# A cross-attention and feed-forward kernel: value matrices placed between score products, weights turned by VectorE in 32x32 blocks

## The chip, the cores and the metric

The kernel runs on one core of one Trainium2 chip. The core has TensorE (PE, whose weight loads are listed apart as PEld), VectorE (DVE), ScalarE (ACT), GpSimd (POOL) and SyncE (SP), and 16 DMA engines that SP, ACT and POOL feed through queues. Time is device microseconds of one execution; the figure is the median of three runs.

## The reference

`x` is 4 batches of 1024 tokens of 512 numbers; `ctx` is 64 context tokens per batch. 16 heads of 64. All is float32.

```python
# attention part, h = layernorm(x)
q, k, v = heads(h @ w_q), heads(ctx @ w_k), heads(ctx @ w_v)
scores = q @ k.T / 8 + causal(-10000)           # 1024 x 64 per head
x = x + tanh(g_xattn) * (softmax(scores) @ v) @ w_o

# feed-forward part, h = layernorm(x); act_qdq: one scale for the whole tensor
h = act_qdq(h)                                  # 16 bits
up   = act_qdq(h @ lpbq(w_up).T)                # w_gate, w_up: 1536 x 512
gate = act_qdq(h @ lpbq(w_gate).T)
gate = act_qdq(gate * u16(sigmoid(gate)))
x = x + tanh(g_ffn) * (act_qdq(gate * up) @ lpbq(w_down).T)
```

`lpbq` takes each run of 32 weights of a row, scales it by its largest absolute value over 7, rounds to integers and scales back.

## The kernel before, in words

**Folding.** The kernel never forms q, k or v of the long side. It computes per batch b a matrix `m_all[b]` (512 x 1024: `w_q` times the keys) and a matrix `vwo[b]` (1024 x 512: values times `w_o`, scaled by tanh). Scores of a token are then its normed row times `m_all[b]`; the attention output is the softmax weights times `vwo[b]`. Each is two halves in two buffers.

**Products by sevens.** The large products take two token tiles (a pair, `q`) at once and a 2x2 split of both sides, in seven products instead of eight. Each side needs sums of its blocks first: of the tokens (`score_left`, L346), of the softmax weights (in `weights_turned`, L616), of `m_all` and `vwo` (`batch_sums(b, k)`, L364: k=0 for `m_all`, k=1 for `vwo`; four DVE operations on 128x1024 numbers, L381 to L386) and of the weights (`weight_sums`, L279).

**Stages.** Set-up loads the weights and computes keys, `m_all` (the loop over head pairs `hp`, with the first pair's tokens turned at hp=7, L482) and values. Then the value-matrix loop (L527): first batches 2 and 3 together, then 0 and 1 together, for each head pair one matrix of each of the two batches, of two 64x64 products on TensorE; the even batch is evicted by ACT (L543), the odd one by DVE (L545). `m_all` and `vwo` of batches 2 and 3 are written to DRAM by POOL (L521, L547) and fetched when needed. `batch_sums(0, 0)` stands before the second round.

Attention is a loop over 16 pairs (L735), four pairs a batch. `scores(q+1)` (L555) runs ahead, seven products into three PSUM banks `sp`, `sq`, `sn`, evicted by ACT and DVE (L576, L578); between them stand the transposes of pair q's softmax weights (L627) and of pair q+2's tokens (L352), by a table `between`/`behind`. Then `softmax(q+1)` on DVE and ACT (L590 to L612), `attend(q)` (L639) with seven products into PSUM tiles `opn` and `oq`, evicted by DVE into the token buffer `xg` (L669, L672, L675), and `renormed` (L680), the second norm with its transposes (L700). After `attend`, at pairs 1 and 3 of a batch, the next batch's `batch_sums` are traced.

In the same loop one chunk (128 rows) of the gate weights per pair is loaded by one DMA from SP and turned into its levels by `dequantized` (L216: reduce, two small steps, two 128x512 products, L221 to L230); chunks 4 to 11 come first and go to DRAM raw (`wg_d`), chunks 0 to 3 stay; pairs 13 and 14 fetch two groups back and prepare four up chunks. The chunks are transposed on TensorE, four 128x128 blocks each (L235), and copied by ACT (L237): gate chunks in pairs 13 to 15, the early up chunks after the last pair, the other eight up chunks in the gate stage.

The gate stage (24 units of seven products, L839, PSUM evicted at L847 to L865 and L956), the up stage, and the down stage (L1448, L1372) follow. A scale over all tokens (`a_x`) stands between attention and gate.

**What sets the order.** Each engine runs its own list in order. The list is made at compile time: a planner takes the earliest traced of the operations that it believes ready, with operations under `high_priority` ahead; TensorE's list follows the source in the attention and gate stages (`manual_schedule`). `keep_in_program_order` puts one operation behind the one traced before it on its engine; `issue_after(ins)` puts a block's operations behind `ins`. Large buffers come from one pool of 20 slots of 8 KB per partition.

```python
ps = ps_mm.tile([P, H], F32, name=f"ps_vo{b}_{hp}", tag="mm")
for j in range(2):
    half = slice(j * D, (j + 1) * D)
    to = j if b % 2 == 0 else 1 - j
```

Here `half` is the half of TensorE's rows that a product reads and `to` the half of its columns that it fills; an even and an odd batch use different quarters.

Of the kernel before, what the change touches and what calls it, by code (L numbers as in the profile page):

```python
# [7 lines left out]
F32 = mybir.dt.float32  # L8
I16 = mybir.dt.int16
# [8 lines left out]
P = 128  # L18
# [9 lines left out]
def kernel(  # L28
# [123 lines left out]
    wg_d = [dram.tile([P, 4, H], F32, name=f"wg_d{k}") for k in range(2)]  # L152
# [63 lines left out]
    def dequantized(pool, src, w, name, in_order=False):  # L216

        nc.sync.dma_start(out=w, in_=src)
        wb = w.rearrange("p (n k) -> p n k", k=QB)
        am = pool.tile([P, NQB], F32, name=f"wam_{name}", tag="wam")  # L220
        ins = nc.vector.tensor_reduce(am, wb, AX.X, ALU.max, apply_absolute_value=True)  # L221
        if in_order:
            tc.keep_in_program_order(ins)
        nc.vector.tensor_scalar(am, am, 1.0 / W_QMAX, 1e-12, ALU.mult, ALU.max)
        inv = pool.tile([P, NQB], F32, name=f"winv_{name}", tag="winv")
        nc.vector.reciprocal(inv, am)
        shape = [P, NQB, QB]
        wi = pool.tile(shape, I16, name=f"wi_{name}", tag="wi", bufs=1)
        nc.vector.tensor_tensor(wi, wb, inv.unsqueeze(2).to_broadcast(shape), ALU.mult)
        nc.vector.tensor_tensor(wb, wi, am.unsqueeze(2).to_broadcast(shape), ALU.mult)  # L230
# [10 lines left out]
    wgT, wuT, wd, wdT, up_chunks = [], [], [], [], []  # L241

    def turned_chunk(psp, w, oc, into, name):

        if oc % 4 == 0:
            into.append(slot([P, HC, 4 * P], f"w{name}T{oc // 4}"))
        cols = slice((oc % 4) * P, (oc % 4 + 1) * P)
        ps = psp.tile([P, 4, P], F32, name=f"wps_{name}{oc}", tag="tr")
        turned(ps, w, into[-1][:, :, cols])

    def up_chunk(psp, w):
        oc = len(up_chunks)
        up_chunks.append(oc)
        turned_chunk(psp, w, oc, wuT, "u")
# [133 lines left out]

    with tc.tile_pool(name="su", bufs=1) as su, tc.tile_pool(
# [88 lines left out]
        for hp in range(HP):  # L478
            if hp + 1 < HP:
                query_turned(hp + 1)  # L480
            else:
                left[0] = score_left(0, centred(0))  # L482
# [40 lines left out]

# [3 lines left out]
        for a in reversed(range(B // 2)):  # L527
            if a == 0:
                for _ in batch_sums(0, 0):
                    pass  # L530
            for hp in range(HP):
                for b in (2 * a, 2 * a + 1):
                    ps = ps_mm.tile([P, H], F32, name=f"ps_vo{b}_{hp}", tag="mm")
                    for j in range(2):
                        half = slice(j * D, (j + 1) * D)
                        to = j if b % 2 == 0 else 1 - j
                        nc.tensor.matmul(
                            ps[to * D : (to + 1) * D, :], vT[half, hp, b * KL : (b + 1) * KL],
                            wo[hp // 4][half, hp % 4, :], start=True, stop=True,
                        )  # L540
                    dst = vwo[b][hp // 4][:, hp % 4, :]
                    if b % 2 == 0:
                        nc.scalar.activation(dst, ps, AF.Copy, scale=tanh_g[0])  # L543
                    else:
                        nc.vector.tensor_scalar(dst, ps, tanh_g[0], None, ALU.mult)  # L545
                    if b > 1 and hp % 4 == 3:
                        nc.gpsimd.dma_start(out=vwo_d[b][hp // 4], in_=vwo[b][hp // 4])  # L547
# [3 lines left out]
    with tc.tile_pool(name="ps_s", bufs=1, space=PSUM) as ps_s, tc.tile_pool(  # L551
# [3 lines left out]
        def scores(q, between):  # L555

            a, b = left.pop(q), right[0][q // QPB]
            e = pa.tile([P, 2, NH, KL], F32, name=f"e{q}", tag="e")
            c = e.rearrange("p i (n h) k -> p i n (h k)", n=2)
            bank = {  # L560
                k: ps_s.tile([P, H], F32, name=f"{k}{q}", tag=k) for k in ("sp", "sq", "sn")
            }
            m1, c12, c22 = c[:, 1, 0], c[:, 0, 1], c[:, 1, 1]
            for k, at, start, dst, other in (
                (1, "sp", True, m1, None), (6, "sq", True, c12, m1), (2, "sp", False, c[:, 0, 0], None),
                (5, "sn", True, c22, m1), (7, "sq", False, c22, c22), (3, "sn", False, c12, c12),
                (4, "sq", False, m1, m1),
            ):
                for h in range(HC // 2):
                    nc.tensor.matmul(  # L570
                        bank[at], a[k][:, h, :], b[k][:, h, :],
                        start=start and h == 0, stop=h == HC // 2 - 1, skip_group_check=True,
                    )
                with tc.high_priority(SOON):
                    if other is None:
                        nc.scalar.copy(dst, bank[at])  # L576
                    else:
                        nc.vector.tensor_tensor(dst, bank[at], other, add)  # L578
                if k in between:
                    between[k]()  # L580
            return e

        def softmax(q, e):

            for i in range(2):
                t = 2 * q + i
                ei = e[:, i]

                if t % TPB == 0:
                    nc.vector.tensor_tensor(  # L590
                        ei, ei, cmask.unsqueeze(1).to_broadcast([P, NH, KL]), ALU.add
                    )
                mx = pa.tile([P, NH], F32, name=f"mx{t}", tag="mx")
                nc.vector.tensor_reduce(mx, ei, AX.X, ALU.max)
                sm = pa.tile([P, NH], F32, name=f"sm{t}", tag="sm")
                if q == 0:

                    nc.vector.tensor_tensor(
                        ei, ei, mx.unsqueeze(2).to_broadcast([P, NH, KL]), ALU.subtract
                    )  # L600
                    nc.scalar.activation(ei, ei, AF.Exp)
                    nc.vector.tensor_reduce(sm, ei, AX.X, ALU.add)
                else:
                    nc.vector.tensor_scalar(mx, mx, -1.0, None, ALU.mult)  # L604
                    for h in range(NH):
                        nc.scalar.activation(  # L606
                            ei[:, h, :], ei[:, h, :], AF.Exp, bias=mx[:, h : h + 1],
                            accum_out=sm[:, h : h + 1],
                        )
                rs = pa.tile([P, NH], F32, name=f"rs{t}", tag="rs")  # L610
                nc.vector.reciprocal(rs, sm)
                nc.vector.tensor_tensor(  # L612
                    ei, ei, rs.unsqueeze(2).to_broadcast([P, NH, KL]), ALU.mult
                )
# [24 lines left out]
        def attend(q, a):  # L639
# [15 lines left out]
            for k, at, start, dst in (  # L655
# [9 lines left out]
                with tc.high_priority(SOON):  # L665
                    if k == 1:
                        nc.scalar.copy(r, bank[at])
                    else:
                        nc.vector.tensor_tensor(dst, bank[at], dst, add)  # L669
# [8 lines left out]
            finished(2 * q, x1)  # L678

# [32 lines left out]
        sg_t, ag, early_up, gate_raw = [], [], [], []  # L712
# [7 lines left out]
        def made_ready(ws, n, src, name, first=0, in_order=False):  # L720

            oc = (len(ws) + first) % n
            if oc % 4 == 0:
                made_in.append(slot([P, min(4, n - oc), H], f"w_{name}{oc}"))
            w = made_in[-1][:, oc % 4, :]
            dequantized(pa, src[oc * P : (oc + 1) * P, :], w, f"{name}{oc}", in_order)
            ws.append(w)

        made_in = []
        two = centred(1)  # L730
        ahead = scores(0, {3: lambda: next_left(1)})
        softmax(0, ahead)
        for _ in batch_sums(0, 1):
            pass
        for q in range(NQ):  # L735
# [15 lines left out]
            if q + 1 < NQ:  # L751
                a = []
                behind = {3: lambda: next_left(q + 2)}
                if q > 0:
                    behind = {5: turn, 3: lambda: (a.append(turn()), next_left(q + 2))}
                ahead = scores(q + 1, behind)
                softmax(q + 1, ahead)
            if q == 0 or q + 1 == NQ:
                turn()
                a = [turn()]  # L760
# [7 lines left out]

            j = q - (NQ - IC // 4)
            if j >= 0:  # L770
                for oc in range(4 * j, 4 * j + 4):
                    turned_chunk(ps_tr, gate_raw[oc], oc, wgT, "g")
# [3 lines left out]
            attend(q, a[0])  # L776
            if b + 1 < B and k in (1, QPB - 1):
                for _ in batch_sums(b + 1, k // 2):
                    pass
# [725 lines left out]
```

## Time and profile before

| | |
|---|---|
| median of 3 runs (lowest, highest) | 1469.0 us (1468.91, 1469.15) |
| the profiled execution | 1467.07 us |
| its span, first to last instruction | 1465.3 us |
| PE, DVE, ACT, POOL busy | 97%, 77%, 47%, 7% |
| TensorE clock granted, mean | 0.995 |
| DMA: moved, mean rate | 240.12 MB, 164 GB/s |
| DMA packets, of them under 512 B | 74,168, 7,396 |

A group's line names the source line, the engine, the operation, out<-in with the count, busy time and mean of one, and the idle time before it with what ended it. A timeline's line gives start and length, the same names, and in brackets the wait before it. TensorE's operations overlap: a group's length holds the tail of its last one, so costs are read from start to next start. A 128x128 transpose is one TensorE instruction, any other float32 product two.

### The profile page before, as it was taken

The numbers are of one execution on the slowest core, as the hardware profiler recorded it, in microseconds if no ns is written. First come the engines' busy times: TensorE is split into PE (matmuls) and PEld (weight loads), VectorE is DVE, ScalarE is ACT, GpSimd is POOL, SyncE is SP. The second block draws the span as 40 slices with busy tenths as digits, with TensorE's granted clock in tenths as the row PEclk, the third lists the DMA queues.
The fourth block names the chain that finished last, engine by engine and source line by source line (L and its number), as shares of the span: only waits on it lengthen the run. The fifth ranks groups of instructions, "written<-read, shape, count | busy, mean of one in ns | idle before, by whom it ended". The sixth has DMA issues, their size and how long they took to land. (4 is left out here: it accounts for less than half of the span.)

```text
span 1465.3 us, 15463 instructions
## 1 busy us (share of the span) xinstructions
PE 1417.2 (97%) x5040; PEld 869.3 (59%) x5040; DVE 1128.0 (77%) x2059; ACT 693.4 (47%) x1746; POOL 96.6 (7%) x191
## 2 busy tenths in 40 slices
PE   8898999999999998999999999999999899999999
PEld 6545766766676674444444444444444448888887
DVE  2976887977988779899956569988888897666632
ACT  2645867767678673111000049977776532222200
POOL 0100000000000001000000000000000101111110
PEclk9999999999999999999999999999999999999999
DMA  9630231431312133664322439958557475554321
GB/s 330 244 130 15 72 115 72 159 129 58 130 47 110 46 130 158 236 223 187 129 86 102 157 127 345 373 216 316 212 210 267 164 282 174 187 187 172 143 72 43
DMA packets 74168, 240.12 MB, mean 164 GB/s; under 512 B 7396, under 2 KB 7652, under 8 KB 68068
## 3 DMA queue, kind: packets, MB, share of 16 engines
q1 hardware_dynamic: 48612, 137.39, 26.8%
q0 software_dynamic: 18560, 76.56, 13.4%
q10 hardware_dynamic: 6912, 25.17, 4.3%
q8 instruction: 39, 0.64, 0.2%
q14 instruction: 45, 0.37, 0.1%
HBM read 130.03 MB, written 109.05 MB: 163 GB/s over the span
## 5 line engine op out<-in xcount | busy, mean ns | idle before, releaser
L606 ACT ACTIVATE e<-e,mx 128x64 f32<-128x64 f32 x480 | 159.7, 339 | 2.2 <-DVE mx L604 2.1
L839 PE MATMUL pqup<-t,wuT 128*128 128x512 f32 x192 | 92.3, 603 | 5.2 <-DVE raw_up L860 2.6
L606 ACT ACTIVATION_READ_ACCUMULATOR e<-e,mx 128x1 f32 x480 | 92.3, 192 | 0.0
L839 PE MATMUL pqgate<-t,wgT 128*128 128x512 f32 x192 | 90.2, 592 | 0.0
L855 ACT COPY raw_gate<-ppgate 128x512 f32<-128x512 f32 x24 | 14.0, 585 | 145.5 <-PE ppgate L839 145.5
L1372 PE MATMUL ep<-wdT,upe 128*128 128x256 f32 x336 | 77.1, 379 | 0.0
L1298 ACT ACTIVATE uie<-upe,inv_up 128x1024 int16<-128x1024 f32 x48 | 53.8, 1145 | 45.8 <-DVE upe L1302 28.7
L661 PE MATMUL oq<-t,eT 128*128 128x256 f32 x256 | 63.7, 393 | 12.0 <-DVE xg L669 8.1
L1372 PE MATMUL eq<-tw,upe 128*128 128x256 f32 x312 | 72.4, 379 | 0.0
L1372 PEld LDWEIGHTS ep<-wdT,upe 128*128 128x128 f32 x336 | 63.8, 190 | 9.1 <-issue 0.5
L1071 ACT ACTIVATE gi<-gt,inv_gate 128x1024 int16<-128x1024 f32 x48 | 54.9, 1143 | 30.3 <-DVE q L1081 30.0
L839 PEld LDWEIGHTS pqup<-t,wuT 128*128 128x128 f32 x192 | 34.7, 189 | 57.0 <-issue 29.7
L839 PE MATMUL ppgate<-xh,wgT 128*128 128x512 f32 x144 | 67.7, 592 | 0.0
L839 PE MATMUL ppup<-xu,wuT 128*128 128x512 f32 x144 | 67.7, 592 | 0.0
L1372 PEld LDWEIGHTS eq<-tw,upe 128*128 128x128 f32 x312 | 59.3, 190 | 8.1
L839 PEld LDWEIGHTS pqgate<-t,wgT 128*128 128x128 f32 x192 | 36.3, 190 | 46.1 <-issue 37.9
L1302 DVE SCALAR_TENSOR_TENSOR upe<-uie,inv_o,gse 128x1024 f32<-128x1024 int16 (+1 forms) x50 | 60.4, 1231 | 3.3 <-ACT uie L1298 3.0
L661 PEld LDWEIGHTS oq<-t,eT 128*128 128x128 f32 x256 | 49.4, 195 | 21.9 <-DVE xg L669 11.0
L570 PE MATMUL sq<-t,xs 128*128 128x512 f32 x128 | 60.3, 593 | 0.0
L629 ACT COPY eT<-ps_e 128x512 f32<-128x512 f32 x64 | 34.3, 588 | 53.5 <-PE ps_e L627 53.5
L967 DVE TENSOR_REDUCE am_gate<-raw_gate 128x1 f32<-128x1024 f32 x48 | 58.2, 1213 | 0.9
L1103 ACT ACTIVATE ar<-raw_up 128x1024 f32<-128x1024 f32 x46 | 48.2, 1047 | 19.1 <-DVE raw_up L1029 19.1
(353 smaller groups left out, 3141.2 us busy)
## 6 DMA issues: line engine op xcount, KB each, us to landing
gate_d<-raw_gate ACTq DMA_DIRECT2D x48, 512.0 KB, 2.6
gt<-gate_d SPq DMA_DIRECT2D x48, 512.0 KB, 4.8
upe<-up_d SPq DMA_DIRECT2D x24, 1024.0 KB, 5.9
up_d<-raw_up POOLq DMA_DIRECT2D x46, 512.0 KB, 3.5
gse<-gsi_d SPq DMA_DIRECT2D x24, 512.0 KB, 4.6
gsi_d<-q SPq DMA_DIRECT2D x44, 256.0 KB, 4.0
xg<-in_x_dram SPq DMA_DIRECT2D x8, 1024.0 KB, 5.2
x_d<-xg POOLq DMA_DIRECT2D x32, 256.0 KB, 2.3
```

The lines of the kernel that those rows point to most:

```text
L570: nc.tensor.matmul(bank[at], a[k][:, h, :], b[k][:, h, :], start=start and h == 0, stop=h == HC // 2 - 1, skip_group_check=True,)
L606: nc.scalar.activation(ei[:, h, :], ei[:, h, :], AF.Exp, bias=mx[:, h : h + 1], accum_out=sm[:, h : h + 1],)
L629: nc.scalar.copy(eT[:, 2 * i + k], ps)
L661: nc.tensor.matmul(bank[at], a[k][:, h, :], b[k][:, h, :], start=start and h == 0, stop=h == HP // 2 - 1, skip_group_check=True,)
L839: nc.tensor.matmul(bank[at], a[k][:, h, :], b[k][:, h, :], start=start and h == 0, stop=h == HC // 2 - 1, skip_group_check=True,)
L855: nc.scalar.copy(r0[:, 0, :], bank["pp"])
L967: nc.vector.tensor_reduce(am_gate[:, u : u + 1], rf, AX.X, ALU.max, apply_absolute_value=True)
L1071: nc.scalar.activation(gi, g, AF.Copy, scale=inv_g)
L1103: nc.scalar.activation(ar, raw[u], AF.Abs)
L1298: nc.scalar.activation(ui, up[:, i, :], AF.Copy, scale=inv_u)
L1302: ins = nc.vector.scalar_tensor_tensor(o[:, i, w], ui[:, w], c_o, gs[:, i, w], ALU.mult, ALU.mult)
L1372: nc.tensor.matmul(bank[at], a[u // 2][k][:, u % 2, q % 2, :], w_of[u // 2][k][:, u % 2, :], start=start and u == 0, stop=u == UPB - 1, sk ...
```

## The change

Three edits, made together.

**Weights.** `turned_chunk` loads a chunk of gate or up weights straight into its place in the turned buffer, by 16 DMAs from SP, each of 32 partitions and runs of 32 numbers, so that 32x32 blocks lie already where their transposed blocks belong; `levels` (the former body of `dequantized`) works on them there, and one DVE transpose, which turns each block of 32x32 in place, ends it. The TensorE transposes and ACT copies of gate and up chunks are gone, also in the gate stage, where the eight up chunks are now at units 2 to 9 instead of 0 to 7. `wg_d` holds turned groups. The down weights are as before.

**Value matrices.** The loop in the set-up makes those of batches 2 and 3 only, with the first pair's tokens turned at hp=2 and `batch_sums(0, 0)` ahead of it. Those of batch 0 are made two at a time behind products 6, 2, 5 and 7 of `scores(0)`, those of batch 1 behind products 1, 6, 2 and 5 of `scores(1)`, in the PSUM tiles that `attend` uses. ACT evicts all but every second one of batch 3. `next_left(1)` moves behind `softmax(0)`; the first pair's softmax weights are turned behind products 3 and 4 of `scores(1)`; `batch_sums(0, 1)` is cut in two, ahead of `softmax(0)` and behind `softmax(1)`.

**Sums.** `batch_sums` after `attend` is issued behind the last eviction of `attend`.

```diff
-    wg_d = [dram.tile([P, 4, H], F32, name=f"wg_d{k}") for k in range(2)]
+    wg_d = [dram.tile([P, HC, 4 * P], F32, name=f"wg_d{k}") for k in range(2)]
...
-    def turned_chunk(psp, w, oc, into, name):
+    def turned_chunk(pool, src, oc, into, name, in_order=False):
         if oc % 4 == 0:
-            into.append(slot([P, HC, 4 * P], f"w{name}T{oc // 4}"))
-        cols = slice((oc % 4) * P, (oc % 4 + 1) * P)
-        ps = psp.tile([P, 4, P], F32, name=f"wps_{name}{oc}", tag="tr")
-        turned(ps, w, into[-1][:, :, cols])
+            into[oc // 4] = slot([P, HC, 4 * P], f"w{name}T{oc // 4}")
+        w = into[oc // 4][:, :, (oc % 4) * P : (oc % 4 + 1) * P]
+        blocks = w.rearrange("p c (b k) -> p c b k", k=BL)
+        rows = src[oc * P : (oc + 1) * P, :].rearrange("(b o) (c a k) -> a o c b k", o=BL, k=BL, c=HC)
+        for a in range(P // BL):
+            for c in range(HC):
+                nc.sync.dma_start(out=blocks[a * BL : (a + 1) * BL, c], in_=rows[a, :, c])
+        levels(pool, blocks, [P, HC, P // BL, QB], f"{name}{oc}", in_order)
+        nc.vector.transpose(w, w)
...
-            else:
-                left[0] = score_left(0, centred(0))
...
-        for a in reversed(range(B // 2)):
-            if a == 0:
-                for _ in batch_sums(0, 0):
-                    pass
-            for hp in range(HP):
-                for b in (2 * a, 2 * a + 1):
...
+        for _ in batch_sums(0, 0):
+            pass
+        def value_matrix(b, hp, ps):
...
+            if b != B - 1 or hp % 2 == 0:
+                nc.scalar.activation(dst, ps, AF.Copy, scale=tanh_g[0])
+            else:
+                nc.vector.tensor_scalar(dst, ps, tanh_g[0], None, ALU.mult)
+
+        for hp in range(HP):
+            if hp == 2:
+                left[0] = score_left(0, centred(0))
+            for b in range(2, B):
+                value_matrix(b, hp, ps_mm.tile([P, H], F32, name=f"ps_vo{b}_{hp}", tag="mm"))
+                if hp % 4 == 3:
+                    nc.gpsimd.dma_start(out=vwo_d[b][hp // 4], in_=vwo[b][hp // 4])
...
+        def values_of(b, n):
+            def some():
+                for _ in range(n):
+                    hp = values_done[b]
+                    values_done[b] += 1
+                    value_matrix(
+                        b, hp, ps_o.tile([P, H], F32, name=f"ps_vo{b}_{hp}", tag=("opn", "oq")[hp % 2])
                     )
+            return some
...
-        ahead = scores(0, {3: lambda: next_left(1)})
+        ahead = scores(0, dict.fromkeys((6, 2, 5, 7), values_of(0, 2)), score_banks(0))
+        firsts = batch_sums(0, 1)
+        next(firsts)
         softmax(0, ahead)
-        for _ in batch_sums(0, 1):
-            pass
+        next_left(1)
...
-                behind = {3: lambda: next_left(q + 2)}
-                if q > 0:
-                    behind = {5: turn, 3: lambda: (a.append(turn()), next_left(q + 2))}
-                ahead = scores(q + 1, behind)
+                behind = {5: turn, 3: lambda: (a.append(turn()), next_left(q + 2))}
+                if q == 0:
+                    behind = {**dict.fromkeys((1, 6, 2, 5), values_of(1, 2)), 3: turn, 4: behind[3]}
+                ahead = scores(q + 1, behind, score_banks(q + 1))
                 softmax(q + 1, ahead)
-            if q == 0 or q + 1 == NQ:
+            if q == 0:
+                next(firsts)
+            if q + 1 == NQ:
...
-            j = q - (NQ - IC // 4)
-            if j >= 0:
-                for oc in range(4 * j, 4 * j + 4):
-                    turned_chunk(ps_tr, gate_raw[oc], oc, wgT, "g")
...
-            attend(q, a[0])
-            if b + 1 < B and k in (1, QPB - 1):
-                for _ in batch_sums(b + 1, k // 2):
-                    pass
+            added = attend(q, a[0])
+            with tc.issue_after(added):
+                if b + 1 < B and k in (1, QPB - 1):
+                    for _ in batch_sums(b + 1, k // 2):
+                        pass
...
             if 0 < q <= IC:
-                made_ready(gate_raw, IC, w_gate, "g", 4, q < 4)
...
+                oc = (q + 3) % IC
+                turned_chunk(pa, w_gate, oc, wgT, "g", q < 4)
+                if oc > 3 and oc % 4 == 3:
+                    nc.gpsimd.dma_start(out=wg_d[oc // 4 - 1], in_=wgT[oc // 4])
...
+                k = q - IC
+                for j in (1, 2) if k == 1 else ():
+                    wgT[j] = slot([P, HC, 4 * P], f"wgTb{j}")
+                    nc.sync.dma_start(out=wgT[j], in_=wg_d[j - 1])
+                if k < 3:
+                    for oc in range(2 * k - 2, 2 * k):
+                        turned_chunk(pa, w_up, oc, wuT, "u")
...
-                if len(ready) > 1 or at >= IC - UPE and ready:
-                    up_chunk(ps_tr, ready.pop(0))
+                if 1 < at < IC - UPE + 2:
+                    oc = UPE + at - 2
+                    turned_chunk(pb, w_up, oc, wuT, "u", True)
```

## The prediction

> **What bounds the kernel now.** I read the totals first, then busy time by stage, then who waited for whom on PE, then PE's and DVE's timelines where PE waits or where the change acts.
>
> The totals, and busy time in the stages (columns: window, length, PE, PEld, DVE, ACT, POOL busy, PE clock, DMA share, GB/s): set-up, value matrices with the first pair, attention, the turn to the feed-forward part, gate, up, down.
>
> ```profile
> PE 1417.2 (97%) x5040; PEld 869.3 (59%) x5040; DVE 1128.0 (77%) x2059; ACT 693.4 (47%) x1746; POOL 96.6 (7%) x191
> ...
> 52.00:124.00 72.00, 59.51 (x296) 31.71 (x297) 58.94 (x117) 41.30 (x116) 3.17 (x6) 0.98 0.36 137
> 124.00:551.00 427.00, 416.65 (x1768) 292.96 (x1768) 347.89 (x723) 297.31 (x1158) 20.92 (x39) 1.00 0.26 93
> 551.00:562.00 11.00, 6.51 (x37) 5.26 (x36) 9.85 (x34) 5.88 (x12) 1.03 (x3) 0.84 0.12 48
> 562.00:862.00 300.00, 299.12 (x722) 133.59 (x721) 233.53 (x435) 35.87 (x62) 10.08 (x18) 1.00 0.43 161
> ```
>
> PE is full in attention and in gate, so there what leaves PE leaves the span. It is not full from 52 to 124 us (12.5 us of idle) nor in the turn at 551. DVE has room in both long stages (81% and 78%).
>
> **Part 1: 24 chunks of gate and up weights turned on DVE.** Removed per chunk: four PE transposes and an ACT copy of 0.59 us. PE's timeline shows where they stand:
>
> ```profile
> 489.28 0.60 PE L235 MATMUL wps_g<-ident,w_g 128*128 128x128 f32 x4
> 490.20 1.62 PE L235 MATMUL wps_g<-ident,w_g 128*128 128x128 f32 x12 [0.32 <-ACT xT L702]
> 491.65 1.89 PE L661 MATMUL opn<-vb,eT 128*128 128x256 f32 x8
> ...
> 518.38 0.60 PE L235 MATMUL wps_g<-ident,wg 128*128 128x128 f32 x4
> 520.08 1.63 PE L235 MATMUL wps_g<-ident,wg 128*128 128x128 f32 x12 [1.10 <-ACT xT L702]
> 521.55 1.89 PE L661 MATMUL opn<-vb,eT 128*128 128x256 f32 x8
> ...
> 552.24 1.55 PE L235 MATMUL wps_u<-ident,w_eu 128*128 128x128 f32 x12
> 557.10 1.94 PE L700 MATMUL ps_xm<-ident,xm 128*128 128x128 f32 x8 [3.30 <-DVE xm L692]
> ```
>
> Gate, start to next start: 491.65 - 489.28 = 2.37; 521.55 - 518.38 = 3.17; a third block, 536.63 to 538.58, 1.95. Sum 7.5. One stall follows: after the second block the last pair's weights are awaited. Its softmax ends at 534.67 and starts 2.4 earlier now; ACT, rid of four copies (2.06 us), brings it to 530.2, while PE, 5.5 earlier, asks for the second half at 529.0. That costs 1.2: **6.3 us**. The early up chunks at 552 stand inside the 3.30 us wait and give PE nothing, but their three copies hold ACT from 552.97 to 554.40 while the square root, whose input is ready at about 553.1, waits behind them; the chain to the first gate product hangs on it: **1.1 us**. In gate, eight blocks of four start 0.44 us ahead of the next product (581.19 to 581.63): **3.5 us**.
>
> Added on DVE: 24 transposes of 128x512. The only near row is one of 128x32:
>
> ```profile
> L396 DVE STREAM_TRANSPOSE row_no<-col_no 128x32 f32<-128x32 f32 x1 | 0.2, 211 | 0.0
> L395 DVE TENSOR_TENSOR_SCAN col_no<-row_no 128x32 f32<-128x32 f32 x1 | 0.2, 202 | 0.0
> ```
>
> It costs what another 128x32 operation costs, so I take what a 128x512 one costs, 0.69 us (L229, 686 ns); the ends are 0.48 (L904 on 128x512) and 16 x 0.211 = 3.4, at which DVE would be full in attention. At 0.69 that is 16.5 us, 12 pairs and two with two chunks, and eight gate units of 12.0 us. The cover is DVE's idle time: attention has 24 to 27 us of DVE in each 30, gate 9.7 us idle between 610 and 646. Price 0; without that cover 0.69 a chunk. The four steps that turn weights into levels (L221 to L230) stay, over the same 512 elements.
>
> Added on SP: 16 DMAs a chunk instead of one, 384 instead of 24, each about 0.43 us of SP (four take 1.76 at 228.89): 6.9 us a chunk, 27.5 for the four chunks of one buffer. Behind them on SP stand the fetches of the next batch (after loads at 95, 229, 330 the next SP issues are at 165, 256.5, 372), so a load group ends just before them. POOL's writes of two turned gate groups replace those of two unturned ones.
>
> Runs are now 128 bytes: a chunk has 2,048 of them and 256 completion packets, 144 packets an engine. The trace has no such transfer. Two queue rows price a packet: q1 (48,612 packets, 137.39 MB, 26.8% of 16 x 1465.3 = 6,283 us) and q10 (6,912, 25.17 MB, 4.3%, 1,008 us) give 0.072 us a packet and 20.3 us a MB; q0 then comes to 2,887 us, measured 13.4%, 3,142. So 0.075 us a run as an estimate, 10.8 us a chunk, 43 a group of four. The group loaded at 228.89 is reduced on DVE from 272.07 to 278.78, its last chunk 50 us later: just in time, price 0. **Against it** speaks the Trainium skill, "DMA: Bandwidth & Descriptors", Specifications: a transfer below 512 B makes the engine read, modify and write. My estimate for that is twice the price, 0.15: 86 us a group, 36 late, and the change loses. No row shows it; I keep the fitted price for the sum and the other for a rival.
>
> **Part 2: value matrices of batches 0 and 1 among the score products.**
>
> ```profile
> 63.72 8.39 PE L537 MATMUL ps_vo<-wo_sb,vT 64*64 64x512 f32 x72
> 72.82 1.09 PE L537 MATMUL ps_vo<-wo_sb,vT 64*64 64x512 f32 x8 [0.71 <-DVE vwo L545]
> ...
> 82.06 1.95 PE L570 MATMUL sp<-m_all,xs 128*128 128x512 f32 x4 [0.95 <-DVE vwo L545]
> ...
> 112.19 1.06 PE L627 MATMUL ps_e<-ident,e 128*128 128x128 f32 x8 [1.90 <-DVE e L612]
> 113.09 1.89 PE L661 MATMUL opn<-vwo,eT 128*128 128x256 f32 x8
> 118.78 2.71 PE L661 MATMUL oq<-t,eT 128*128 128x256 f32 x8 [3.80 <-DVE eT L634]
> ```
>
> Waits there: 2.78 for the first pair's tokens before 59 us, 2.12 + 0.95 for evictions, 0.86 + 1.90 + 3.80 for softmax and sums: 12.4; and after the 3.80 the next 16 products take 5.2 us, not 3.45: 1.8 of lost clock. Against it: an even and an odd batch use different quarters of the array and run four at once (72 starts in 8.39: two matrices in 0.86). Dealt out, neighbours are of one batch, in the same two quarters: 0.86 each, 16 x 0.43 = 6.9 more. Eight groups switch the array between 128 and 64 rows twice at about 0.1: 1.6. ACT now evicts 12 of the 16 early matrices and ends about 2.0 after PE. The second pair's tokens are turned behind the first softmax on DVE's list, so its second product may wait 0 to 2.6; I take 1.2. These matrices issue no DMA; wo and vT hold three buffers some 30 us longer, and the first pair's tokens now need one while POOL's writes of m_all (issued at 62.87) drain. Net 12.4 + 1.8 - 6.9 - 1.6 - 2.0 - 1.2 = **2.5 us**, between -1.5 and +5.
>
> **Part 3: the batch sums queued behind the pair's last eviction.** Five waits of PE for xg stand where they ran: 0.20, 0.26, 2.86, 1.75, 2.86. DVE shows how much is theirs:
>
> ```profile
> 440.34 0.68 DVE L675 TENSOR_TENSOR xg<-xg,r 128x512 f32<-128x512 f32 x1
> 440.95 1.22 DVE L381 TENSOR_TENSOR t<-vb 128x1024 f32<-128x1024 f32 x1
> 442.08 0.42 DVE L669 TENSOR_TENSOR xg<-oq,xg 128x256 f32<-128x256 f32 x1
> ```
>
> Between L675 and the awaited L669 stands one sum, 1.13; the rest is statistics and L612, which stay. So 0.20 + 0.26 + 1.14 + 1.11 + 1.13 = 3.8. At 324.74, after 2.86, eight products take 3.65, not 1.89: 1.8 of clock. The Trainium skill ("TensorE: Matmul & The Clock Gate", Part 1) lets the clock fall after an idle window of about 3.4 us; by that only the 3.80 wait loses clock and this part gives 1.8 less. The row decides. The sums issue no DMA and move into the next score products, where an eviction behind one is (1.2 + 0.69 + 0.2) - 1.72 = 0.37 late, six times: 2.2. Net **3.4 us**.
>
> **Sum.** 6.3 + 1.1 + 3.5 + 2.5 + 3.4 = 16.8. The profiled execution took 1467.07 (span 1465.3 and 1.8 around it), 1.9 under the median of 1469.0; I take the difference off the median: **1452**.
>
> **Rivals.**
> 1. DVE sets the pace in attention. For it: 26 to 27 us busy of 30 in several windows, and an order fixed at compile time. Against: no PE wait of over 0.4 us there but those above. All 14 pairs lose their transposes' time or little waits of that size, 14 x 0.69 = 9.7: **1462**.
> 2. The re-laid order also takes the waits that I left (1.2, 2.0, 1.2, 2.2, and 4.1 of Part 3): up to 10.7 more, half of it likely: **1445**.
> 3. Slower: weights come late in attention. The place is the group loaded at 229 us, whose reductions stand in DVE's fixed order between evictions. At 0.15 us a run it is 86 - 50 = 36 late, 32 after DVE's slack of some 4: **1484**. It decides from 0.123 us a run (576 packets an engine: 71 us, 21 late, 17 lost). Against: the fit says 0.075.
> 4. Nothing measurable: gains and losses cancel, **1469**.
>
> **How the numbers follow.** Chances: forecast 0.60 (1446 to 1458), rival 1 0.16, rival 2 0.12, rival 3 0.09, rival 4 0.03. Within 0.2% (2.9 us) of 1469 a measurement of this kernel tells nothing. Faster 0.60 + 0.16 + 0.12 = 0.88, same 0.03, slower 0.09. The range 1442 to 1464 leaves out rivals 3 and 4 and the tails of 1 and 2, some 0.18.
>
> **What would show it.** PE x4944, DVE x2071, ACT x1734; 126,000 packets, 62,300 under 512 B; STREAM_TRANSPOSE of 128x512 at 0.69; gate 3.5 us shorter; the first product on gate about 7 us earlier from the attention blocks alone; no wait of 3.80 before the first oq; value matrices in 0.86 each; q1 at 42 to 43%. Wrong if DVE waits for DMA at the weights' reductions, if a transpose takes over 1.2 us, or if PE in attention waits for DVE more than 8 us in all.

## The result, and the profile after

The changed kernel takes 1501.4 us (median; 1500.6 to 1505.7) where the kernel before takes 1469.0: ratio 1.0229, 95% interval 1.0215 to 1.0243. The prediction was 1452, with a range up to 1464: wrong in sign, by 49 us.

The totals of the profile after, then the stages (columns as in the prediction). The window 430 to 490 is one of two in attention where PE is not full, 590 to 890 is gate:

```profile
PE 1427.6 (95%) x4944; PEld 864.2 (58%) x4944; DVE 1136.0 (76%) x2071; ACT 688.4 (46%) x1734; POOL 97.7 (7%) x191
...
250.00:310.00 60.00, 59.86 (x249) 40.72 (x248) 50.26 (x99) 43.80 (x172) 2.72 (x5) 1.00 0.45 150
310.00:370.00 60.00, 44.40 (x182) 30.62 (x181) 46.51 (x95) 39.80 (x159) 2.16 (x4) 0.91 0.22 71
430.00:490.00 60.00, 45.83 (x182) 29.19 (x180) 49.88 (x104) 42.13 (x193) 2.71 (x5) 0.93 0.30 88
590.00:890.00 300.00, 294.47 (x675) 129.25 (x676) 236.85 (x441) 31.94 (x55) 10.86 (x18) 0.98 0.44 162
```

Work left PE as counted (x4944), but PE is idle for some 15 us in two stretches of 60, and its clock falls there. Who PE waited for, from 60 to 600 us (total, times, longest), longest first:

```profile
PE ps_xm L725 <- ACT xm L712: 23.0, 2, 11.5
PE oq L685 <- DVE xg L693: 4.5, 4, 1.9
PE ps_e L651 <- DVE r_c L177: 4.5, 1, 4.5
PE ps_xn L361 <- ACT xn L349: 4.2, 2, 2.8
PE ps_xm L725 <- DVE xm L717: 4.1, 1, 4.1
```

No PE wait of 11.5 us existed before (the longest from 60 to 600 us was 3.8). Where the time was lost, by the start of each pair's first product on the value matrices (opn) and of the first product on gate and on up, in us of each profiled execution:

| start of | before | after | after minus before | step |
|---|---|---|---|---|
| pair 1 | 145.59 | 149.94 | 4.35 | +4.35 |
| pair 7 | 313.08 | 317.66 | 4.58 | +0.2 |
| pair 8 | 345.49 | 362.38 | 16.89 | **+12.3** |
| pair 11 | 430.89 | 448.23 | 17.34 | +0.5 |
| pair 12 | 461.65 | 492.45 | 30.80 | **+13.5** |
| pair 13 | 491.65 | 521.37 | 29.72 | -1.1 |
| pair 14 | 521.55 | 548.51 | 26.96 | -2.8 |
| pair 15 | 538.58 | 569.19 | 30.61 | +3.7 |
| gate | 561.08 | 590.96 | 29.88 | -0.7 |
| up | 849.07 | 883.59 | 34.52 | +4.6 |

The rest is equal to 0.2 us (34.3 at the end). So two pairs carry 25.8 of the 34.3 us. Pairs 7 and 11 are pairs that end with batch sums. PE's timeline at the first of the two places (after):

```profile
346.46 1.36 PE L361 MATMUL ps_xn<-ident,xn 128*128 128x128 f32 x8 [2.79 <-ACT xn L349]
347.65 1.88 PE L412 MATMUL s<-t,xs 128*128 128x512 f32 x4
349.37 0.60 PE L725 MATMUL ps_xm<-ident,xm 128*128 128x128 f32 x4
361.47 1.12 PE L725 MATMUL ps_xm<-ident,xm 128*128 128x128 f32 x4 [11.50 <-ACT xm L712]
```

PE turns the first of two xm tiles at once and waits 11.5 us for the second. DVE before that, same execution (the sums are L390 to L395; the norm's chain runs from L172 to L185):

```profile
332.16 0.17 DVE L318 BATCH_NORM_AGGREGATE mv<-st_b 128x2 f32<-128x6 f32 x1
332.25 1.19 DVE L390 TENSOR_TENSOR t<-vb 128x1024 f32<-128x1024 f32 x1
...
338.16 1.22 DVE L395 TENSOR_TENSOR t<-vb,t 128x1024 f32<-128x1024 f32 x1
339.30 0.69 DVE L420 TENSOR_TENSOR e<-s,e 128x512 f32<-128x512 f32 x1
339.90 0.16 DVE L172 TENSOR_SCALAR ve_b<-mv 128x4 f32<-128x4 f32 x1
...
344.70 0.23 DVE L185 SCALAR_TENSOR_TENSOR off<-mv,rstd 128x4 f32<-128x4 f32 x2
```

And ACT: the first xm as soon as off is there, the second behind the softmax's 32 exponentials:

```profile
344.88 0.81 ACT L712 ACTIVATE xm<-xg,off,rstd 128x512 f32<-128x512 f32 x1 [0.54 <-DVE off L185]
345.60 1.50 ACT L349 ACTIVATE xn<-xg,off,rstd 128x512 f32<-128x512 f32 x2
...
349.05 0.35 ACT L448 ACTIVATE e<-e,mx 128x64 f32<-128x64 f32 x1
...
360.62 0.80 ACT L712 ACTIVATE xm<-xg,off,rstd 128x512 f32<-128x512 f32 x1
```

Before, in the same pair, off was ready 6.0 us after the first score product (335.98 against 329.95), and both xm ran ahead of the exponentials:

```profile
335.75 0.23 DVE L185 SCALAR_TENSOR_TENSOR off<-mv,rstd 128x4 f32<-128x4 f32 x2
...
335.95 0.81 ACT L687 ACTIVATE xm<-xg,off,rstd 128x512 f32<-128x512 f32 x1
...
339.89 0.81 ACT L687 ACTIVATE xm<-xg,off,rstd 128x512 f32<-128x512 f32 x1
...
349.31 0.35 ACT L606 ACTIVATE e<-e,mx 128x64 f32<-128x64 f32 x1
```

After, it is ready 13.5 us after it (344.93 against 331.46).

### The profile page after: what moved, and what is told of

Its sections match the earlier page's. It is cut to its first block, busy times and chain, and to the rows that moved or that the text cites. A ratio compares the mean times of both kernels' runs of the same rounds, so it can differ in the third digit from the quotient of the medians.

```text
span 1499.6 us, 15723 instructions
## 1 busy us (share of the span) xinstructions
PE 1427.6 (95%) x4944; PEld 864.2 (58%) x4944; DVE 1136.0 (76%) x2071; ACT 688.4 (46%) x1734; POOL 97.7 (7%) x191
## 3 DMA queue, kind: packets, MB, share of 16 engines
q1 hardware_dynamic: 100452, 137.41, 27.2%
## 4 chain that ended last, share of the span: by engine, by line
PE 72%; DVE 13%; ACT 5%; issue 5%; DMA 3%; SPq 1%; POOL 0%; DVEq 0%; ACTq 0%; POOLq 0%
PE s L412 11%; PE pqgate L851 8%; PE eq L1374 7%; PE opn L685 6%; PE ppgate L851 5%; PE pngate L851 5%; PE en L1374 5%; PE ep L1374 5%; PE pqup L851 4%; PE oq L685 4%; PE ps_d L1450 3%; PE pnup L851 2%; ACT e L448 2%; DMA up_d<-raw_up 2%; SPq L261 1%
## 5 line engine op out<-in xcount | busy, mean ns | idle before, releaser
L420 DVE TENSOR_TENSOR e<-s,e 128x512 f32<-128x512 f32 x80 | 55.0, 688 | 60.5 <-PE s L412 60.1
L412 PE MATMUL s<-t,xs 128*128 128x512 f32 x192 | 91.6, 600 | 2.2 <-DVE xs L366 2.2
L867 ACT COPY raw_gate<-ppgate 128x512 f32<-128x512 f32 x24 | 14.1, 586 | 150.0 <-PE ppgate L851 143.1
L851 PE MATMUL pqgate<-t,wgTb 128*128 128x512 f32 x128 | 62.2, 609 | 4.6 <-DVE raw_gate L877 4.2
L859 ACT COPY raw_gate<-ppgate 128x512 f32<-128x512 f32 x24 | 14.1, 586 | 109.6 <-PE ppgate L851 71.4
L412 PE MATMUL s<-m_all,xs 128*128 128x512 f32 x128 | 59.7, 598 | 1.2 <-DVE vwo L608 0.9
L412 PEld LDWEIGHTS s<-t,xs 128*128 128x128 f32 x192 | 35.2, 191 | 42.1 <-issue 39.1
L412 PE MATMUL s<-mb,xs 128*128 128x512 f32 x128 | 58.9, 592 | 0.0
```

The lines of the kernel that those rows point to most:

```text
L412: nc.tensor.matmul(bank[at], a[k][:, h, :], b[k][:, h, :], start=start and h == 0, stop=h == HC // 2 - 1, skip_group_check=True,)
L851: nc.tensor.matmul(bank[at], a[k][:, h, :], b[k][:, h, :], start=start and h == 0, stop=h == HC // 2 - 1, skip_group_check=True,)
```

## Experiments: the three parts one by one

Theory A: the held-back sums (Part 3) push the norm's chain back on DVE, and ACT's order, fixed at compile time, then has xm behind the exponentials. Theory B: the work of Part 1 on DVE does it. Theory C: only both together.

**Part 3 alone.**

```
-            attend(q, a[0])
-            if b + 1 < B and k in (1, QPB - 1):
-                for _ in batch_sums(b + 1, k // 2):
-                    pass
+            added = attend(q, a[0])
+            with tc.issue_after(added):
+                if b + 1 < B and k in (1, QPB - 1):
+                    for _ in batch_sums(b + 1, k // 2):
+                        pass
```

> The kernel before with the batch sums held back behind the pair's last eviction and nothing else. Theory A (the held-back sums are the cause: on DVE they run between the pair's statistics and the chain that makes rstd and off, the chain ends some 9 us later, and ACT's fixed order then has the normalized token tile xm behind the next 32 exponentials, so PE waits about 11.5 us for it): in the instruction order of this kernel three pairs have an xm behind the exponentials, where the changed kernel has two, which cost it 12.3 and 13.5; 3 x 12.9 less some 1.5 of waits removed is 37, so about 1506, and three PE waits of some 11.5 us for xm. Theory B (the work that turning the weights adds on DVE delays the chain): no such wait, 1465.6 as in the forecast. Theory C (only the two together do it): the same 1465 to 1469.

Measured: 1519.6, ratio 1.0341 (1.0314 to 1.0369). PE's waits:

```profile
PE ps_xm L701 <- ACT xm L688: 34.3, 3, 11.5
PE ps_xn L352 <- ACT xn L340: 8.6, 5, 2.3
PE oq L661 <- DVE xg L669: 5.0, 4, 1.9
```

Three waits of 11.5, as the order said. Theories B and C fall: no weight is turned on DVE here. The 1506 was 14 too low: pairs 7, 9 and 11 are 13.5, 14.8 and 15.2 us longer than before, 43.5 of 50, and the pair behind each is 1.6 to 2.1 longer too. In pair 7, off is ready 11.5 us after the first score product (340.70 against 329.16), so of the 7.5 us of delay in the changed kernel the sums make 5.5; the other 2 come only there, where two steps of Part 1 on DVE (L232 and L263, 1.4 together) stand inside the chain. The waits for xg did shrink, from 8.4 to 5.0, which is what Part 3 does well. (Of the 8.6 for xn, 2.8 stand in the set-up, as in the kernel before.)

**Parts 1 and 2 without Part 3.** The changed kernel with the diff above undone:

```
-            added = attend(q, a[0])
-            with tc.issue_after(added):
+            attend(q, a[0])
```

> The changed kernel with the batch sums issued as before, not held back. Theory A: both 11.5 us waits for xm are gone, and with them 12.3 + 13.5 = 25.8 us; the waits for xg of 1 to 3 us come back, about 1.5: 1501.4 - 25.8 + 1.5 = 1477. Theory B: the two waits stay, about 1500. Theory C: 1477 as A.

Measured: 1472.4, ratio 1.0023 (1.0012 to 1.0033), no wait for ACT's xm. 29 of the 32 us are Part 3's; A is right, and its 1477 was 5 too high.

**Part 1 alone**, and **Part 2 alone**: the kernel before with those hunks of the change's diff and no others. Their core, first for Part 1, then for Part 2:

```
+                nc.sync.dma_start(out=blocks[a * BL : (a + 1) * BL, c], in_=rows[a, :, c])
+        levels(pool, blocks, [P, HC, P // BL, QB], f"{name}{oc}", in_order)
+        nc.vector.transpose(w, w)
```

```
-        ahead = scores(0, {3: lambda: next_left(1)})
+        ahead = scores(0, dict.fromkeys((6, 2, 5, 7), values_of(0, 2)), score_banks(0))
...
+                    behind = {**dict.fromkeys((1, 6, 2, 5), values_of(1, 2)), 3: turn, 4: behind[3]}
```

> The kernel before with gate and up weights turned on DVE and nothing else. Theory A, by the steps that the trace of the changed kernel shows: -1.1 and -2.8 where two blocks of transposes left attention, +3.6 before the last pair, -0.7 in the turn, +4.6 in gate: 1469 + 3.6, about 1473, with one PE wait of some 4 us before the last pair and one of some 4 us in gate, seven units in. Theory B: two waits of 11.5 us for xm as well, about 1495. The forecast's own sum for this part was 1458.

> The kernel before with the value matrices of batches 0 and 1 among the score products and nothing else. From the trace of the changed kernel, whose second pair starts 4.35 us later than before and keeps that distance for six pairs: 1473. The forecast's own sum for this part was 1466.5 (between 1464 and 1470.5).

Measured: Part 1 1469.4, ratio 1.0003 (0.9991 to 1.0014); Part 2 1469.8, 1.0007 (0.9997 to 1.0017). Neither can be told from no change; the 1473 expected of both was 3 to 4 too high. Part 1's two waits came as expected (4.5 us before the last pair, 4.6 in gate, in its third unit). Part 2's second pair, in a profiled execution of 1467.0 us that is among the fastest of its 20, starts at 147.29, 1.7 later than before, not 4.35. PE runs the same instructions there in the changed kernel; the rest of its 4.35 is clock lost behind two waits (1.7 at 57.8 us, 1.6 at 101.7), less 0.7 by which it started earlier.

## Experiments: is it ACT's order, or the late chain?

**xm first.** In the changed kernel:

```
+                with tc.high_priority(SOON):
                     nc.scalar.activation(
                         xn, xg[g][:, i, :], AF.Identity, bias=off2[:, t : t + 1],
```

> The changed kernel with one thing more: the activation on ACT that makes xm is given the same high priority as the evictions, so that in the instruction order no pair has an xm behind its 32 exponentials; the sums stay held back and the chain to rstd and off stays late. If ACT's order is what costs (theory A): the two waits of 11.5 us and some 2.5 us of clock behind them go, 1501.4 - 25.5, about 1476. If the late chain itself costs (the other theory): PE still waits some 5 us or more at the same two places and for xn as well, 1488 or more.

Measured: 1478.4, ratio 1.0064 (1.0046 to 1.0082), no wait for ACT's xm. ACT's order is what cost most. The late chain still costs: 1478.4 against 1472.4 without Part 3, and PE now waits for xn, which stands behind xm:

```profile
PE ps_xn L361 <- ACT xn L349: 7.0, 2, 3.5
```

**Chain first.** The kernel before with Part 3, and `norm_of(pa, parts, f"b{g}")` with what makes `parts` moved ahead of the held-back sums:

```
             added = attend(q, a[0])
+            if q % 2 == 1 and q + 1 < NQ:
...
+                norm_of(pa, parts, f"b{g}")
             with tc.issue_after(added):
```

> The kernel before with the batch sums held back behind the pair's last eviction, and the chain of rstd and off put ahead of them in the program; in its instruction order no pair has an xm behind the exponentials. Theory A: the three waits of 11.5 us are gone, 1519.6 - 51 or less; the forecast's gain for the held-back sums (3.4 us) then shows, 1465. If holding the sums back brings nothing even then: 1468.5. If they still delay the chain: over 1480.

Measured: 1465.1, ratio 0.9979 (0.9971 to 0.9987). With the chain ahead of them the held-back sums gain 3.3 us; the prediction had 3.4. PE's waits for xg fall by 3.4, the slow products behind the wait at 324.74 (1.8) are gone, and two waits for xn come in, 1.8. So both gains that the prediction counted for Part 3 came. That the sum agrees so well is in part luck: its term of loss (2.2, late evictions) was another than the one that came. Whether the chain moved alone, without held-back sums, gains anything was not run.

## Experiments: what Part 1 loses in gate

In the changed kernel four gate products, at the end of the third unit and the start of the fourth, take 13.7 us instead of 6.9 (627.54 to 641.23). PE, DVE and SP there:

```profile
627.54 1.88 PE L851 MATMUL pngate<-t,sg 128*128 128x512 f32 x4
633.61 3.78 PE L851 MATMUL pqgate<-t,wgTb 128*128 128x512 f32 x4 [4.19 <-DVE raw_gate L877]
637.18 2.50 PE L851 MATMUL ppgate<-xT,wgTb 128*128 128x512 f32 x4
```

```profile
632.20 0.75 DVE L914 TENSOR_SCALAR xh<-xh,inv_x 128x1024 f32<-128x1024 f32 x1 [4.00 <-DMA xh<-xh_d]
632.87 0.68 DVE L877 TENSOR_TENSOR raw_gate<-pqgate,raw_gate 128x512 f32<-128x512 f32 x1
```

```profile
614.33 11.36 SPq L261 DMA_DIRECT2D wuT<-in_L_ffn_w_up_dram  x22
625.79 1.21 SPq L985 DMA_DIRECT2D xh<-xh_d  x2
627.22 15.81 SPq L261 DMA_DIRECT2D wuT<-in_L_ffn_w_up_dram  x19
```

The awaited eviction (L877) stands on DVE behind an operation on the next tokens (xh), whose fetch stands on SP behind 22 small weight DMAs: 0.52 to 0.83 us each, not the 0.43 of the prediction.

**xh from another queue**, on Part 1 alone:

```
-                    nc.sync.dma_start(out=xT[g], in_=xh_d[g])
+                    nc.gpsimd.dma_start(out=xT[g], in_=xh_d[g])
```

> Only the weights turned on DVE, as in the run of part 1 alone (1469.4), and the next tokens' fetch in gate (xh) issued from POOL's queue instead of SP's. If the fetch was late because 16 weight DMAs a chunk stand ahead of it on SP: PE's wait of 4.6 us for raw_gate and the 2.5 us of slower products after it go, 1469.4 - 7 = 1462.5. If it was late because its buffer came free late: no change, 1469.

Measured: 1471.8, ratio 1.0022 (1.0014 to 1.0031): a miss. DVE no longer waits for xh, and PE waits all the same, 5.5 us. ACT's waits from 560 to 700 us name the next one:

```profile
ACT raw_gate L845 <- DMA wuT<-in_L_ffn_w_up_dram: 16.5, 2, 8.8
```

A copy on ACT waits for weight DMAs that it has no use for. In the compiled program SP's and ACT's DMAs take eight completion semaphores in turn, and each waits until the last user of its semaphore has landed. So ACT's write of gate_d waits for a small weight DMA on SP, and the next copy from PSUM stands behind that write:

```profile
608.88 0.33 ACTq L958 DMA_DIRECT2D gate_d<-raw_gate  x1
609.24 0.58 ACT L845 COPY raw_gate<-ppgate 128x512 f32<-128x512 f32 x1 [8.82 <-DMA wuT<-in_L_ffn_w_up_dram]
```

The trace's records show it: what this write takes is complete at 599.5 us; its semaphore was last taken by a weight DMA that SP issued at 607.12 and that landed at 608.71; the write is issued at 608.88.

**One DMA a chunk**, on Part 1 alone:

```
-        for a in range(P // BL):
-            for c in range(HC):
-                nc.sync.dma_start(out=blocks[a * BL : (a + 1) * BL, c], in_=rows[a, :, c])
+        nc.sync.dma_start(out=w, in_=rows)
```

> Only the weights turned on DVE, but each chunk fetched with one DMA of 512-byte runs instead of 16 of 128-byte runs; what is left out is the placing of the blocks, so the gate and up weights stand in a wrong order and the output is not the reference's. If the price of the runs and issues lies only in SP's queue in gate: as with xh on another queue, 1462.5, and attention as long as with 16 DMAs. If the short runs cost DMA time that shows: attention shorter by more than 2 us as well, under 1460. If neither matters: 1469.

The rows are read in their own order here (`"p (c k) -> p c k"`): the placing of the blocks is left out, the output is not the reference's, and only the time counts. Measured: 1466.4, ratio 0.9984 (0.9975 to 0.9993), 3.0 less than with 16 DMAs where 7 was expected. Gate, from its first product to up's first, takes 285.6 us against 292.9 with 16 DMAs, so the whole gain that was expected is there. Attention isn't shorter but longer (391.6 us from pair 1 to pair 15, 388.5 with 16 DMAs), so no cost of the short runs shows there; of these 3.1, 1.7 is clock lost behind a wait at 324.8, and the rest stays open.

**The up chunks' DMAs from POOL**, on Part 1 alone:

```
-                nc.sync.dma_start(out=blocks[a * BL : (a + 1) * BL, c], in_=rows[a, :, c])
+                queue.dma_start(out=blocks[a * BL : (a + 1) * BL, c], in_=rows[a, :, c])
...
-                    turned_chunk(pb, w_up, oc, wuT, "u", True)
+                    turned_chunk(pb, w_up, oc, wuT, "u", True, nc.gpsimd)
```

> Only the weights turned on DVE (1469.4 alone), with the 128 small DMAs of the eight up chunks in gate issued from POOL instead of SP. SP's and ACT's DMAs share eight completion semaphores in turn, so a write of gate values on ACT's queue waits until an earlier small weight DMA has landed, and ACT's next copy stands behind that write: by this theory gate gets as short as with one DMA a chunk, 1469.4 - 7.4 = 1462. If the short runs themselves slow the other transfers: no change, 1469. If POOL's issues come to hold up its own writes of xq and ts: over 1472.

Measured: 1461.9, ratio 0.9952 (0.9935 to 0.9969), faster than both kernels, by half a per cent than the one before. Gate takes 287.0, and no wait of ACT names wuT any more (one of 4.6 us names a DMA of the down weights). The 1462 expected came. Both the queue and the shared semaphores were taken away here; the run with xh on POOL shows that the tokens' place in SP's queue alone was not it.

## Experiments: the last pair, and all together

In Part 1 alone PE waits 4.5 us for the last softmax (the row names r_c; what the product needs is e, whose scaling, just ahead of r_c on DVE, ends when the wait does). The 32 exponentials start 4.7 us after the last score product (1.6 before): DVE has a turned chunk ahead of the maxima, and ACT two xm ahead of them. **Maxima first**, in the last pair only:

```
+            with tc.high_priority(SOON if q + 1 == NQ else 0):
                 nc.vector.tensor_reduce(mx, ei, AX.X, ALU.max)
```

> Only the weights turned on DVE, and in the last pair alone the maxima of the softmax get the priority of the evictions, so that the 32 exponentials start ahead of two xm on ACT. If the last pair's wait of 4.5 us comes from the exponentials' late start (4.7 us after the last score product, 1.6 in the kernel before): it falls to about 1.5 and the slow products behind it go, 1469.4 - 4 = 1465.4. If the 32 exponentials of 0.33 us and the scaling behind them bound it wherever they start: 1469.

Measured: 1469.5, ratio 1.0004 (0.9995 to 1.0013): no gain. Half of the step happened, and was given back:

```profile
531.20 1.07 PE L638 MATMUL ps_e<-ident,e 128*128 128x128 f32 x8 [2.31 <-DVE mv L318]
...
544.17 1.13 PE L672 MATMUL oq<-t,eT 128*128 128x256 f32 x4 [2.09 <-DVE xg L680]
```

The wait falls from 4.5 to 2.3, and the last pair starts 3.9 us earlier after the one before it. But weight sums and an am_x that were overtaken now stand in front of the next evictions: a wait of 2.1 us comes in, and from the pair's start to gate it takes 23.9 us instead of 22.5. That leaves 2.4 us in this profiled execution which the medians don't show; where they go isn't settled (here the step from pair 11 to 12 was 1.7 us longer, after a wait that cost clock).

**POOL and maxima first together**, then **with Part 3 as well** (chain ahead of the sums, xm first):

> Only the weights turned on DVE, with both of the mends (up chunks' DMAs in gate on POOL, maxima of the last pair first). If both theories hold the gains add: 1469.4 - 7.4 - 4 = 1458, faster than the kernel before by 0.7%. If neither: 1469.

> The same with the sums held back as well, the norm chain ahead of them in the program and xm at the evictions' priority, so that no pair has an xm behind its exponentials. If holding the sums back is worth the 3.3 us that it gave alone with the chain ahead: 1455. If DVE, with the weights' work between, still ends the chain late and PE waits for xn some 3 us at two or three places, as with xm's priority alone: 1462 or more.

Measured: 1463.5, ratio 0.9962 (0.9947 to 0.9977), no better than with POOL alone; and 1465.7, 0.9986 (0.9977 to 0.9994). The gain of 3.3 us from the held-back sums is not there once the weights' work is on DVE: in attention PE waits for xn 2.4 us at 342.0 and 1.9 at 460.4, where it did not without the held-back sums, and loses 1.7 of clock behind each; that is the second reading.

## Why the prediction was wrong, step by step

- **Part 3, forecast 3.4 us of gain, measured +50 alone and +29 on top of the others.** The step that failed is "move into the next score products, where an eviction behind one is ... 0.37 late, six times: 2.2". It asked which evictions stand behind a moved sum on DVE. Behind the four sums also stands the norm's chain, on that ACT's xm, and on that PE's fixed order. The chain ends 7.5 us later in its pair, 5.5 with Part 3 alone. That costs some 6 us over the whole kernel even with xm first (1478.4, against 1472.4 without Part 3); ACT makes a wait of 11.5 of it, twice or three times, because 32 exponentials stand in between. Why the compiled order puts xm there in some pairs and not in others stays open. Rival 1 had "an order fixed at compile time" and priced it at 0.69 a pair.
- **Part 1 in gate, forecast -3.5.** The eight transposes' 0.44 each did leave (the distance shrinks by it from unit to unit). The step that failed is "16 DMAs a chunk instead of one, 384 instead of 24", which enters the sum with nothing: the prediction asked what stands behind SP's weight DMAs in attention and not in gate, where the tokens' fetch does, and it did not ask whether DMAs on two engines share a semaphore. In place of the 3.5 gained, 4.6 were lost in the changed kernel and 5.0 in Part 1 alone.
- **Part 1 in attention, forecast -6.3 and -1.1.** The first two blocks left 2.4 and 2.8 (2.37 and 3.17 forecast). The third is the step "That costs 1.2": the removed transposes had covered the last softmax, which also starts 3.1 us later after the last score product, and the interval grows by 4.1: PE waits 4.5 there, not 1.2. In the turn nothing was gained.
- **Transposes on DVE, 0.69.** Right:

```profile
L263 DVE STREAM_TRANSPOSE wgT<-wgT 128x512 f32<-128x512 f32 x12 | 8.4, 696 | 0.1
```

- **Runs of 128 bytes, 0.075 us as an estimate.** Far too dear, and rival 3 with 0.15 more so. Queue 1 after:

```profile
q1 hardware_dynamic: 100452, 137.41, 27.2%
```

51,840 packets more than before and 243 us more of the engines' time (27.2% of 16 x 1499.6 against 26.8% of 16 x 1465.3): 0.005 us each. The rule of the Trainium skill ("DMA: Bandwidth & Descriptors", Specifications) that a transfer under 512 bytes is read, modified and written has no price here that shows.
- **Part 2, forecast -2.5 with -1.5 to +5 of gain.** Measured +1.0 of loss (-0.4 to +2.5 by its interval), within its range. The term for the second pair's tokens, 1.2, was 2.4 (0.2 and 2.2); a group of two matrices and its product takes 3.78 us (77.68 to 81.46), 0.14 more than forecast, eight times; and of the 2.78 us of waits before 59 us, 1.2 came back as a wait for m_all where the moved transposes had stood.

## What to carry to other kernels

When work is held back or moved on an in-order engine, list everything queued behind its new place, above all short chains that end in another engine's queue: there a delay of a few us can become a whole softmax if the late instruction falls behind a long block. A transfer cut into many small DMAs costs by its issues and by the semaphores that it takes in turn with other engines' DMAs, more than by its bytes. Try each part of a joint change alone: here one part cost 50 us alone, two were nothing, and with one queue changed Part 1 was the fastest version.

## What the runs showed of the hardware that was not expected

The clock that is lost after a wait of PE isn't set by the wait's length alone. The same wait, before the same eight products, in Part 1 with POOL's queue, at two places:

```profile
119.02 1.99 PE L670 MATMUL oq<-t,eT 128*128 128x256 f32 x8 [3.80 <-DVE eT L643]
...
438.69 3.78 PE L670 MATMUL oq<-t,eT 128*128 128x256 f32 x8 [2.87 <-DVE xg L678]
442.26 3.14 PE L670 MATMUL opn<-vb,eT 128*128 128x256 f32 x8
```

3.80 us of wait cost nothing here and 1.8 in the kernel before; 2.87 cost 3.0 here, and 1.8 and nothing at the two places of that length in the kernel before.

The granted clock shows what decides. In all 14 traces it is 1.00 or 0.50, and it changes only at the marks of a grid of 3.41 us, which lies elsewhere in each execution. PE's busy time between such marks (columns: window, length, PE busy, clock, DMA share, GB/s), in the kernel before at the 3.80, then with POOL's queue at the 3.80 and at the 2.87:

```profile
116.50:119.91 3.41, 1.13 (x5) 1.00 0.01 2
119.91:123.33 3.42, 3.42 (x10) 0.50 0.00 0
...
113.68:117.09 3.41, 1.53 (x8) 1.00 0.22 34
117.09:120.51 3.42, 1.49 (x7) 1.00 0.24 37
...
434.53:437.95 3.42, 1.29 (x6) 1.00 0.86 335
437.95:441.36 3.41, 2.67 (x6) 0.50 0.78 260
441.36:444.77 3.41, 3.41 (x9) 0.50 0.24 60
```

Where a mark cuts the 3.80 us in two, both windows are busy for 0.44 and 0.45 of their length and nothing is lost. Where most of the wait falls into one window (0.33 and 0.38 busy), the next one is granted half. Over the 14 traces, all 77 full-speed windows with PE busy for less than 0.41 were followed by a half-speed one, and 7 of the other 5,796, at 0.43 to 0.64. Of the 114 half-speed windows, the 41 with PE busy for 0.80 or less were followed by another one, the 73 others by full speed: that is why the 2.87, which ends inside the second window, cost two. A wait of 2.2 us among Part 2's products, with the same instructions on PE, cost 1.6 in the changed kernel and in Parts 1 and 2 together (busy 0.37 and 0.40) and nothing in Part 2 alone (0.50).

The Trainium skill ("TensorE: Matmul & The Clock Gate", Part 1) says that the window of about 3.4 us that watches activity is free-running, and that the number of slow products at a kernel's start varies by run with it. The grid agrees with that; but where it has the clock fall after an idle window, here a window with PE busy for up to 0.41 was idle enough. For a forecast it means that a wait of 2 to 4 us carries 0 to 3 us of clock, by where it falls on a grid that isn't known beforehand, and that steps of 1 or 2 us between two profiled executions, as Part 2's 4.35 against 1.7, are not the kernel's.
